# A row of attention scores by way of DRAM, and a group of transposes moved behind four additions

## The chip, the cores and the metric

The kernel runs on one core of a Trainium2 chip. The metric is the device time of one execution in microseconds; the median of three runs of the kernel before is 2945.22 us (2944.97 to 2953.04). TensorE is the matmul engine (PE in the profile), VectorE is DVE, ScalarE is ACT, GpSimd is POOL, and SyncE (SP) issues most of the transfers.

## The reference

The program is two layers over 64 graphs of 256 nodes with 256 features. Layer 0 is a graph attention network, layer 1 a relational attention with 8 heads. Everything is float32.

```python
def _gat(h, adj, W, a, F):
    Wh = h @ W
    e = leaky_relu(Wh @ a[:F] + swapaxes(Wh @ a[F:], 1, 2), 0.2)
    att = softmax(where(adj > 0, e, -9e15), axis=1)
    return att @ Wh

# layer 0
h = _gat(_gat(x, adj, W1, a1), adj, W2, a2)          # first and second attention
h = layernorm(x + h)
x = layernorm(h + relu(h @ w_ff1 + b_ff1) @ w_ff2 + b_ff2)
# layer 1
attn = softmax(q @ k.T / sqrt(32))                   # 8 heads; q, k, v projected from x
out = sum(attn * (adj == r) @ v_r for r in range(4)) @ Wo + bo
x = layernorm(x + out)
x = layernorm(x + gelu(x @ W1 + b1) @ W2 + b2)
```

The change concerns one term of the second attention: `Wh @ a[F:]` is one number for each node, and the scores need it as a row, the same in all 128 partitions, with the 512 nodes of two graphs along the free dimension.

## The kernel before

Graphs are worked on in pairs, 32 groups in all. A group's rows lie in SBUF as 128 partitions by 4 blocks of 128 nodes (two blocks for each graph). The main loop calls `turn` 32 times; a turn works on three groups at once, each at another stage: group y does its attention of layer 1 and its second feed-forward, group x its first feed-forward, and group z, two behind y, both attentions of layer 0. TensorE so always has a product of some group to do. In 30 of the 32 turns there is a group z; the first two groups go through these stages in a prologue.

The order of the instructions is written out by hand for TensorE, SP, VectorE and ScalarE inside a turn (`manual_schedule`); GpSimd's order, and the seam between two turns on VectorE, are left to the planner. Products of the feed-forwards and projections are done with seven block products in place of eight: `hidden_seven` holds the first half of a feed-forward. Its steps are named by a digit, the number of the product, and a or b, the half of the hidden blocks. A step puts a product into a PSUM bank and then takes it from there: the first product that goes to a quarter of h is copied by ScalarE (L954), the second is added by VectorE (L951). Steps c, d and s apply the Gelu to a finished quarter on ScalarE (L960); step 4 applies it straight from PSUM. `HiddenOut` holds the second half: sums of quarters on VectorE (L1020, tiles eq and eaq), then the products L1034, whose additions into y are L1042.

Around the change, the second half of a turn runs so. TensorE does the products of the second hidden layer of y. VectorE meanwhile finishes the moments of group x (L865, L866), takes the additions L951, applies a scale and a shift to y (L903, L906), and then transposes group x's normalised rows in blocks of 32 by 32 (`normed_features`, L717, four instructions). The blocks are afterwards put where they belong by twelve transfers on SP and four copies on GpSimd (L726), which gives hT, the features by nodes, of the next turn's layer 1. Only then come the last four additions of h (steps 7a, 7b, 3a, 3b).

After step 4b, `second_scores` makes the row: `score_rows` transposes a column of hp, broadcast to 128 columns, with four matmuls against the identity (L781), one for each block of nodes, into a PSUM bank. ScalarE makes the raw scores from it, one instruction for each block (L799: row plus the node's own number as the bias), VectorE the leaky step (L807), ScalarE the exponential (L810), VectorE masks and sums (L814, L818), and ScalarE scales hp (L830), which the products of the second attention (L850, ygp) use. Between these stand the output products of y: product 1, which needs a finished quarter of h, then product 5, which needs the first sum, and so on. The next turn begins with differences of hT on VectorE (L1069, tile tq) and the projections (L1102).

Pools hand out buffers: "g" has six PSUM banks, "es" two buffers in SBUF of 4 KB a partition, used by sums of exponentials (L1140) and reciprocals (L1160). `to_broadcast` reads one column many times over without copying it.

Of the kernel before, what the change touches and what calls it, by code (L numbers as in the profile page):

```python
# [9 lines left out]
F32 = mybir.dt.float32  # L10
# [6 lines left out]
P = 128  # L17
# [368 lines left out]
def narrow_path(  # L386
# [13 lines left out]
    nc = tc.nc  # L400
    B, N, F = x.shape
# [7 lines left out]
    T = G * NB  # L409
    TN = G * N  # L410
# [6 lines left out]
    const = ctx.enter_context(tc.tile_pool(name="const", bufs=1))  # L417
    io = ctx.enter_context(tc.tile_pool(name="io", bufs=2))
    work = ctx.enter_context(tc.tile_pool(name="work", bufs=2))
    psum = ctx.enter_context(tc.tile_pool(name="psum", bufs=1, space=PSUM))  # L420
    ctx.enter_context(nc.allow_non_contiguous_dma(reason="vectors, once"))

    def bank(name):
        return psum.tile([P, 512], F32, tag="g", name=name, bufs=6)


    Q = P // 32
# [255 lines left out]
    rows = work.tile([P, T, 2 * F], F32, tag="v", name="rows", bufs=1)  # L683
# [10 lines left out]
    def behind(*names):  # L694

        stack = ExitStack()
        for n in names:
            stack.enter_context(tc.issue_after(mark[n].ins))
        return stack
# [7 lines left out]
    def with_ones(hT):  # L707

        nc.gpsimd.memset(hT[KB - 1][one], 1.0)
        return hT  # L710

    def normed_features(u, l, xn, natural=False, copied=(), later=False):


        yt = work.tile([P, Q, KB, T, 32], F32, tag="yt", name=f"yt{u}_{l}", bufs=1)
        for t in range(T):
            mark["transposed"] = nc.vector.transpose(  # L717
                yt[:, :, :, t].rearrange("p q k r -> p k q r"),
                xn[:, t].rearrange("p (k q c) -> p k q c", k=KB, c=32))
        if natural:  # L720
            hT = work.tile([P, KB, TN], F32, tag="hT", name=f"hT{u}_{l}")
            to = hT.rearrange("c k (t a r) -> c (k t) a r", a=Q, r=32)
            for q in reversed(range(Q)):
                for a in range(Q):
                    move = nc.gpsimd.tensor_copy if q == a else nc.sync.dma_start
                    move(to[q * 32:(q + 1) * 32, :, a], yt[a * 32:(a + 1) * 32, q].rearrange("c k t r -> c (k t) r"))  # L726
            return with_ones([hT[:, k] for k in range(KB)])
        hT = work.tile([P, Q, KB, T, 32], F32, tag="hT", name=f"hT{u}_{l}")
        n, moves = 0, []
        for q in range(Q):  # L730
            for a in range(Q):
                to, at = hT[q * 32:(q + 1) * 32, a], yt[a * 32:(a + 1) * 32, q]
                if q == a:
                    nc.gpsimd.tensor_copy(to, at)  # L734
                else:
                    if n not in copied:
                        nc.sync.dma_start(to, at)
                    elif later:
                        moves.append((to, at))
                    else:  # L740
                        nc.scalar.copy(to, at)
                    n += 1
        hT = [hT[:, :, k].rearrange("p a t r -> p t a r") for k in range(KB)]
        return (hT, iter(moves)) if later else hT
# [32 lines left out]
    def score_rows(u, l, wh, c):  # L777

        rows = bank(f"rows{u}_{l}")
        for t in range(T):  # L780
            nc.tensor.transpose(rows[:, t * P:(t + 1) * P],  # L781
                                wh[:, t, c:c + 1].to_broadcast([P, P]), ident)
        return rows

    class Softmax:
# [83 lines left out]
    def norm(u, l, y, blocks=range(T), mv=None, rest=range(NB, T)):  # L869

        n, t0 = f"{u}_{l}_{blocks[0]}", blocks[0]
        bt = slice(t0, t0 + len(blocks))
        mv = moments(u, l, y, blocks if mv is None else rest, mv)
        rs = work.tile([P, T], F32, tag="rs", name=f"rs{n}")
        nm = work.tile([P, T], F32, tag="nm", name=f"nm{n}")
        nc.gpsimd.tensor_scalar(rs[:, bt], mv[:, bt, 1], EPS, 0.0, op0=ALU.add, op1=ALU.add)  # L876
        nc.gpsimd.tensor_tensor(rs[:, bt], rs[:, bt], mhalf[:, bt], ALU.pow)  # L877
        if l == 3:
            nc.gpsimd.tensor_add(high[:, bt], high[:, bt], mv[:, bt, 0])
        return blocks, mv, rs, nm  # L880

    def offsets(blocks, mv, rs, nm):
        bt = slice(blocks[0], blocks[0] + len(blocks))
        mark["offset"] = nc.vector.scalar_tensor_tensor(nm[:, bt], mv[:, bt, 0], -1.0, rs[:, bt], op0=ALU.mult, op1=ALU.mult)  # L884

    def applied_norm(y, blocks, mv, rs, nm, part=None, gpsimd=False):
        if part is None:
            offsets(blocks, mv, rs, nm)
        for t in part or blocks:
            if gpsimd:  # L890
                nc.gpsimd.tensor_scalar(y[:, t, :], y[:, t, :], rs[:, t:t + 1], nm[:, t:t + 1],
                                        op0=ALU.mult, op1=ALU.add)
                continue
            mark["normed"] = nc.scalar.activation(y[:, t, :], y[:, t, :], AF.Identity,  # L894
                                                  bias=nm[:, t:t + 1], scale=rs[:, t:t + 1])

    def affine(y, g_, b_):

        times(y, g_)
        plus(y, b_)  # L900

    def times(y, g_):
        nc.vector.tensor_mul(y, y, g_[:, None, :].to_broadcast(list(y.shape)))  # L903

    def plus(y, b_):
        nc.vector.tensor_add(y, y, b_[:, None, :].to_broadcast(list(y.shape)))  # L906
# [142 lines left out]
    def out_sums(u, l):  # L1049
        two = [work.tile([P, HPB, NB * N], F32, tag=t, name=f"{t}q{u}_{l}") for t in ("e", "ea")]  # L1050
        return [t[:, :, i * N:(i + 1) * N] for t in two for i in range(2)]
# [137 lines left out]
        d = g[z]  # L1189
        d["xp"] = projected(z, d["xT"], blocks, d.get("xp"))  # L1190

    def first_scores(z):
        d = g[z]
        d["m"] = Softmax(z, 0, d["xp"], score_rows(z, 0, d["xp"], F + 2), F + 3)

    def second_scores(z):
        d = g[z]
        d["m"] = Softmax(z, 1, d["hp"], score_rows(z, 1, d["hp"], F), F + 1)

    def first_softmax(z):  # L1200
        first_scores(z)
# [61 lines left out]
    def stored(u, y, bt):  # L1263
        b = slice(G * u + bt.start // NB, G * u + bt.stop // NB)
        nc.sync.dma_start(out[b].rearrange("b (c p) f -> p (b c) f", p=P), y[:, bt, :])
# [47 lines left out]
    def turn(y_, x_, z, rest=None):  # L1313
        Y, X, Z = (g.get(u) for u in (y_, x_, z))
        hT, y = Y["hT"], Y["y"]
        quads = [(b, m) for b in range(G) for m in range(KB)]
        p = Projections(y_, hT)
        q, k_, v = p.qk[:, :, 0], p.qk[:, :, 1], p.v
# [44 lines left out]
        with order:  # L1363
# [227 lines left out]
            second = hidden_seven(y_, 1, hT, w1s, b1, AF.Gelu, Y, tt.rearrange("p a n -> p (a n)"), bool(X))  # L1591
# [6 lines left out]
            if not X:  # L1598
# [2 lines left out]
                half(1)  # L1601
                second("t")
            if Z:
                second("2a 1a")
                n = norm(x_, 1, X["y"], mv=n, rest=range(NB + 1, T))
                second("2b 1b ca 6a")
                offsets(*n)
                applied_norm(X["y"], *n, [0])
                applied_norm(X["y"], *n, [2, 3], True)
                second("5a")  # L1610
                applied_norm(X["y"], *n, [1])
                affine(y, rg3, rb3)
                second("6b 5b cb")
                X["hT"] = normed_features(x_, 1, X["y"], natural=True)
                second("7a 7b sa sb 3a da 3b db 4a 4b")
            else:
                if X:
                    n = norm(x_, 1, X["y"], mv=n, rest=range(NB + 1, T))
                second("2a 1a 2b 1b" if X else "2b 1b")
                if not X:  # L1620
                    with behind("added"):
                        affine(y, rg3, rb3)
                second("5a 5b")
                if waiting:
                    times(waiting[0][1], rg4)
                second("3a 3b")
                if X:
                    offsets(*n)
                    applied_norm(X["y"], *n, [0])
                    applied_norm(X["y"], *n, [1])  # L1630
                    applied_norm(X["y"], *n, [2, 3], True)
                second("6a 6b ca cb da db 7a 7b")
                if waiting:
                    plus(waiting[0][1], rb4)
                    stored(*waiting.pop(), slice(0, T))
                if X:
                    X["hT"] = with_ones(to_features(X["y"], f"h2T{x_}", (nc.vector.tensor_copy,) * 2))
                second("sa sb 4a 4b")
            if y_ >= NG - 2:
# [5 lines left out]
                else:  # L1645
                    for _ in pieces:
                        pass
                return
            second_scores(z)
            out = HiddenOut(y_, 1, y, h1, w2s, out_sums(y_, 1))  # L1650
            out.product(1)
            out.sums(1, 2)
# [229 lines left out]
```

## Time and profile before

| What | Value |
|---|---|
| Median of three runs | 2945.22 us |
| The profiled execution's own time | 2946.93 us |
| Its span, first to last instruction | 2945.3 us |
| TensorE busy | 2921.1 us, 99% |
| VectorE busy | 2609.6 us, 89% |
| ScalarE busy | 1898.9 us, 64% |
| GpSimd busy | 624.9 us, 21% |
| Row transposes of the second attention (L781, from hp) | 128 matmuls, 19.4 us busy, all 32 groups |
| Transposes of features (L717) | 364 in all, median 402 ns |
| hT transfers behind them (L726) | 360, 609 ns of issue each |
| Granted TensorE clock | 0.998 of full speed |

A line of a group of instructions names the line of the code, the engine, the operation, the tile written and those read, the shapes and the count; after the bar come the busy time, the mean of one instruction in ns, and the idle time before them. In a timeline a line begins with the start in us from the start of the span and the time that the merged instructions cover; at its end, in brackets, stands the idle time before it and what ended it. A matmul of float32 operands is two hardware instructions, so 8 products of the code are "x16"; a transpose is one. Matmuls overlap, so a TensorE instruction's price is the distance between starts, not its duration.

### The profile page before, as it was taken

To read this page: it belongs to the slowest core of one execution; us is meant where nothing else is said; L and a number is where in the kernel's file an instruction comes from. 1 tells how busy PE (TensorE), PEld (TensorE's weight loads), DVE (VectorE), ACT (ScalarE), POOL (GpSimd) and SP (SyncE) were. 2 spreads that over 40 slices of the span, in tenths; PEclk is the share of its full clock that TensorE was granted. 3 is DMA by queue.
4 is the path that set the end of the run, shared out by engine and by line. 5 is a ranking of instruction groups with operands and counts; after the bars stand their busy time and mean duration, and the time that the engine had idled before them with its cause. 6 is when DMAs were issued, how large, how long until landed. Compare 5 with 4: busy or idle time off the path is not lost.

```text
span 2945.3 us, 58649 instructions
## 1 busy us (share of the span) xinstructions
PE 2921.1 (99%) x22206; PEld 2502.4 (85%) x22206; DVE 2609.6 (89%) x5027; ACT 1898.9 (64%) x3985; POOL 624.9 (21%) x931
## 2 busy tenths in 40 slices
PE   9999999999999999999999999999999999999998
PEld 7788888888888888888888888888888888888876
DVE  5889899988989898999889898989998898989886
ACT  5566666676666666666766766666667667666653
POOL 3312211122121122111221211221112212112210
PEclk9999999999999999999999999999999999999999
DMA  5011111111111111111111111111111111111000
GB/s 153 13 31 32 38 32 34 24 40 32 37 29 23 38 32 38 32 33 24 40 33 37 29 23 38 32 39 32 33 24 40 32 37 30 23 38 32 17 9 16
DMA packets 408020, 99.27 MB, mean 34 GB/s; under 512 B 357834, under 2 KB 407220, under 8 KB 407732
## 3 DMA queue, kind: packets, MB, share of 16 engines
q1 hardware_dynamic: 406332, 94.13, 14.8%
q8 instruction: 178, 2.92, 0.4%
q0 software_dynamic: 1056, 1.05, 0.1%
q14 instruction: 110, 0.90, 0.1%
q10 hardware_dynamic: 344, 0.28, 0.0%
HBM read 56.78 MB, written 16.78 MB: 25 GB/s over the span
## 4 chain that ended last, share of the span: by engine, by line
PE 97%; DVE 1%; ACT 1%; DMA 0%; issue 0%; POOL 0%; POOLq 0%; DVEq 0%; ACTq 0%
PE yf L1034 27%; PE h1a L942 15%; PE h1b L942 12%; PE po L1151 8%; PE v L1102 6%; PE qk L1102 6%; PE sp L1123 4%; PE hpp L839 4%; PE ygp L850 4%; PE xpp L772 4%; PE yop L850 4%; PE zo L1154 2%; PE rows L781 1%; DMA first<-in_adj_dram 0%; ACT h L960 0%
## 5 line engine op out<-in xcount | busy, mean ns | idle before, releaser
L1132 ACT ACTIVATE e<-sp 128x512 f32<-128x512 f32 x512 | 270.9, 612 | 71.2 <-issue 43.8
L1136 DVE TENSOR_TENSOR ea<-e,aT 128x1024 f32<-128x1024 f32 x256 | 310.1, 1213 | 1.6 <-ACT e L1132 1.6
L894 ACT ACTIVATE y<-y,nm,rs 128x256 f32<-128x256 f32 x442 | 235.0, 592 | 57.5 <-DVE nm L884 56.7
L951 DVE TENSOR_TENSOR h<-h1a,h 128x512 f32<-128x512 f32 x293 | 197.1, 680 | 81.4 <-PE h1a L942 81.3
L954 ACT COPY h<-h1b 128x512 f32<-128x512 f32 x293 | 175.4, 599 | 124.9 <-PE h1b L942 123.1
L960 ACT ACTIVATE h<-h,cols 128x256 f32<-128x256 f32 x512 | 222.4, 502 | 36.8 <-DVE h L951 32.5
L734 POOL COPY hT<-yt 32x256 f32<-32x256 f32 x244 | 211.3, 866 | 145.0 <-DVE yt L717 132.4
L1089 ACT COPY qk<-qk 128x512 f32<-128x512 f32 x128 | 74.3, 580 | 234.7 <-PE qk L1102 233.9
L865 DVE BATCH_NORM_STATS2 st<-y 128x6 f32<-128x256 f32 x512 | 208.6, 408 | 5.6
L876 POOL TENSOR_SCALAR rs<-mv 128x4 f32<-128x4 f32 (+1 forms) x134 | 41.5, 310 | 805.8 <-DVE mv L866 439.0
L1042 DVE TENSOR_TENSOR y<-yf,y 128x256 f32<-128x256 f32 x448 | 184.9, 413 | 29.7 <-PE yf L1034 29.7
L960 ACT ACTIVATE h<-h1a,cols 128x256 f32<-128x256 f32 x256 | 102.7, 465 | 132.4 <-PE h1a L942 132.3
L1164 POOL TENSOR_TENSOR low<-low,rq 128x16 f32<-128x16 f32 x64 | 13.9, 217 | 810.4 <-DVE rq L1163 802.6
L906 DVE TENSOR_TENSOR y<-y,rb 128x1024 f32<-128x1024 f32 x126 | 163.0, 1294 | 2.2
L1141 DVE TENSOR_TENSOR es<-e 128x1024 f32<-128x1024 f32 x128 | 155.4, 1214 | 0.0
L903 DVE TENSOR_TENSOR y<-y,rg 128x1024 f32<-128x1024 f32 x126 | 152.8, 1213 | 0.0
L877 POOL TENSOR_TENSOR rs<-rs,mhalf 128x4 f32<-128x4 f32 (+1 forms) x134 | 139.5, 1041 | 8.3
L1123 PE MATMUL sp<-qk 32*128 32x256 f32 x2048 | 138.3, 394 | 0.0
L942 PE MATMUL h1a<-tt,wf 128*128 128x256 f32 x512 | 137.6, 392 | 0.0
L1151 PE MATMUL po<-e,v 128*32 128x256 f32 x2048 | 135.5, 382 | 0.0
L1151 PE MATMUL po<-ea,v 128*32 128x256 f32 x2048 | 134.5, 379 | 0.0
L717 DVE STREAM_TRANSPOSE yt<-y 128x256 f32<-128x256 f32 x364 | 128.3, 407 | 0.9 <-ACT y L894 0.7
(288 smaller groups left out, 7728.3 us busy)
## 6 DMA issues: line engine op xcount, KB each, us to landing
hT<-yt SPq DMA_DIRECT2D x666, 32.0 KB, 1.8
y<-in_x_dram SPq DMA_DIRECT2D x32, 512.0 KB, 5.2
xq<-in_x_dram SPq DMA_DIRECT2D x240, 64.0 KB, 2.1
aq<-in_adj_dram SPq DMA_DIRECT2D x240, 64.0 KB, 2.2
out_dram<-y SPq DMA_DIRECT2D x30, 512.0 KB
wf<-in_L_gnn_w_ff_dram SPq DMA_DIRECT2D x2, 1024.0 KB, 8.5
w<-in_L_gnn_W_dram SPq DMA_DIRECT2D x2, 1024.0 KB
first<-in_adj_dram POOLq DMA_DIRECT2D x2, 512.0 KB, 9.7
```

The costliest lines, as they stand in the source:

```text
L734: nc.gpsimd.tensor_copy(to, at)
L850: nc.tensor.matmul(ps[:, i * F:(i + 1) * F], lhs(t, k), rhs(b, k), start=(k == 0), stop=(k == n - 1))
L865: nc.vector.bn_stats(st[:, t, :], y[:, t, :])
L894: mark["normed"] = nc.scalar.activation(y[:, t, :], y[:, t, :], AF.Identity, bias=nm[:, t:t + 1], scale=rs[:, t:t + 1])
L942: nc.tensor.matmul(ps[:, i * N:(i + 1) * N], w_[:, f * P:(f + 1) * P], m, start=first and i == 0, stop=True, skip_group_check=True)
L960: nc.scalar.activation(y, y if ps is None else ps[:, i * N:(i + 1) * N], func, bias=bi[:, f:f + 1])
L1034: nc.tensor.matmul(s.ps[n][:, i * F2:(i + 1) * F2], a[:, k, i * P:(i + 1) * P], w_[:, k, :], start=n in (1, 2, 5) and i == 0 and k == 0, s ...
L1102: nc.tensor.matmul(ps[:, i * N:(i + 1) * N], l, r, start=n in (1, 2, 5) and i == 0, stop=True, skip_group_check=True)
L1123: nc.tensor.matmul(ps[a][:, j * N:(j + 1) * N], k_[hp, m, j0:j0 + P], q[hp, m, b * N:(b + 1) * N], start=True, stop=True)
L1132: nc.scalar.activation(e[:, a, :], ps[a], AF.Exp, scale=isd)
L1136: nc.vector.tensor_tensor(ea[:, a:a + 2, :], e[:, a:a + 2, :], ab[:, None, :].to_broadcast([P, 2, NB * N]), ALU.mult)
L1151: nc.tensor.matmul(po[hp, m * N:(m + 1) * N], vs[:, hp], w[:, a, j * N:(j + 1) * N], start=(n == 0), stop=(n == len(terms) - 1))
```

## The change

The second attention's row no longer comes from TensorE. A new helper, `line_rows`, is called at the beginning of the second hidden layer of y, one hidden layer earlier than the row is used. One VectorE transpose turns the column of hp, broadcast to 32, in blocks of 32 by 32, so that partitions 0, 32, 64 and 96 each hold 32 nodes of every block. A transfer writes these to a line in DRAM in 16 pieces of 128 bytes, in the order of the nodes; a second reads the line back into all 128 partitions. The row is then a tile in SBUF from the pool's "es" buffers, and `second_scores` takes it in place of making its own. The prologue's two groups, and the first attention of all groups, still use `score_rows`.

The second part moves `normed_features` of group x, its four transposes with their twelve transfers and four copies, from before step 7a to after step 3b, behind the last addition of h.

```diff
+    dram = ctx.enter_context(tc.tile_pool(name="dram", bufs=2, space=bass.MemoryType.DRAM))
...
+    def line_rows(u, l, wh, c):
+        line = dram.tile([T, Q, 32], F32, tag="line", name=f"line{u}_{l}")
+        rows = work.tile([P, TN], F32, tag="es", name=f"rows{u}_{l}")
+        turned_ = rows[:, :T * 32].rearrange("p (t r) -> p t r", r=32)
+        nc.vector.transpose(turned_, wh[:, :, c:c + 1].to_broadcast([P, T, 32]))
+        nc.sync.dma_start(line.rearrange("t q r -> q t r"), turned_[::32])
+        nc.sync.dma_start(rows, bass.AP(tensor=line.tensor, offset=line.offset, ap=[[0, P], [1, TN]]))
+        return rows
...
-    def second_scores(z):
+    def second_scores(z, rows=None):
         d = g[z]
-        d["m"] = Softmax(z, 1, d["hp"], score_rows(z, 1, d["hp"], F), F + 1)
+        d["m"] = Softmax(z, 1, d["hp"], score_rows(z, 1, d["hp"], F) if rows is None else rows, F + 1)
...
             if Z:
+                rows1 = line_rows(z, 1, Z["hp"], F)
                 second("2a 1a")
...
                 second("6b 5b cb")
+                second("7a 7b sa sb 3a da 3b db")
                 X["hT"] = normed_features(x_, 1, X["y"], natural=True)
-                second("7a 7b sa sb 3a da 3b db 4a 4b")
+                second("4a 4b")
...
-            second_scores(z)
+            second_scores(z, rows1)
```

More of the change, by code (lines that the diff above doesn't have):

```diff
@@ L1190, in project, with first_scores @@
         d["xp"] = projected(z, d["xT"], blocks, d.get("xp"))
-    def first_scores(z):
+    def first_scores(z, rows=None):
         d = g[z]
-        d["m"] = Softmax(z, 0, d["xp"], score_rows(z, 0, d["xp"], F + 2), F + 3)
-    def second_scores(z):
+        d["m"] = Softmax(z, 0, d["xp"], score_rows(z, 0, d["xp"], F + 2) if rows is None else rows, F + 3)
+    def second_scores(z, rows=None):
         d = g[z]
-        d["m"] = Softmax(z, 1, d["hp"], score_rows(z, 1, d["hp"], F), F + 1)
+        d["m"] = Softmax(z, 1, d["hp"], score_rows(z, 1, d["hp"], F) if rows is None else rows, F + 1)
     def first_softmax(z):
```

## The prediction

> **What bounds the kernel now.** I read the page first: busy shares, then the chain that ended last, then the row transposes' own group.
>
> ```profile
> PE 2921.1 (99%) x22206; PEld 2502.4 (85%) x22206; DVE 2609.6 (89%) x5027; ACT 1898.9 (64%) x3985; POOL 624.9 (21%) x931
> ...
> PE 97%; DVE 1%; ACT 1%; DMA 0%; issue 0%; POOL 0%; POOLq 0%; DVEq 0%; ACTq 0%
> ```
>
> ```profile
> L781 PE MATMUL rows<-ident,hp 128*128 128x128 f32 x128 | 19.4, 273 | 0.1
> ```
>
> TensorE is the chain. Whatever leaves its queue is gained unless it then waits. The 273 ns of a row transpose is its latency; they overlap, so the price must be read from distances. For that I took the timeline of one turn in the middle, engine by engine. TensorE, around the four row transposes:
>
> ```profile
> 1417.31 1.89 PE L942 MATMUL h1a<-tt,w 128*128 128x256 f32 x8
> 1419.04 1.89 PE L942 MATMUL h1b<-hT,w1s 128*128 128x256 f32 x8
> 1420.77 1.89 PE L942 MATMUL h1a<-tt,w 128*128 128x256 f32 x8
> 1422.49 0.60 PE L781 MATMUL rows<-ident,hp 128*128 128x128 f32 x4
> 1422.93 1.95 PE L1034 MATMUL yf<-w,h 128*128 128x128 f32 x16
> 1424.72 1.95 PE L1034 MATMUL yf<-w2t,eq 128*128 128x128 f32 x16
> ```
>
> The first three lines are steps 7, 3 and 4 of the second hidden layer (a and b each); then the row; then output products 1 and 5. There is no gap. VectorE, ScalarE and the transfer queue in the same stretch:
>
> ```profile
> 1411.53 0.18 DVE L866 BATCH_NORM_AGGREGATE mv<-st 128x2 f32<-128x6 f32 x1
> 1412.40 0.69 DVE L951 TENSOR_TENSOR h<-h1a,h 128x512 f32<-128x512 f32 x1 [0.70 <-PE h1a L942]
> ...
> 1416.53 1.47 DVE L906 TENSOR_TENSOR y<-y,rb 128x1024 f32<-128x1024 f32 x1
> 1417.92 1.41 DVE L717 STREAM_TRANSPOSE yt<-y 128x256 f32<-128x256 f32 x4
> 1419.26 1.24 DVE L951 TENSOR_TENSOR h<-h1a,h 128x512 f32<-128x512 f32 x2
> 1420.43 1.26 DVE L951 TENSOR_TENSOR h<-h1b,h 128x512 f32<-128x512 f32 x2
> 1423.27 1.23 DVE L1020 TENSOR_TENSOR eq<-h 128x1024 f32<-128x1024 f32 x1 [1.57 <-ACT h L960]
> ```
>
> ```profile
> 1419.94 3.30 ACT L960 ACTIVATE h<-h,cols 128x256 f32<-128x256 f32 x8 [1.04 <-DVE h L951]
> 1423.14 1.53 ACT L960 ACTIVATE h<-h1a,cols 128x256 f32<-128x256 f32 x4
> 1424.57 1.56 ACT L799 ACTIVATE s<-rows,hp 128x256 f32<-128x256 f32 x4
> ```
>
> ```profile
> 1409.92 0.39 SPq L441 DMA_DIRECT2D y<-in_x_dram  x1
> 1419.39 8.35 SPq L726 DMA_DIRECT2D hT<-yt  x12
> 1429.75 5.32 SPq L449 DMA_DIRECT2D aq<-in_adj_dram  x8
> ```
>
> The reader should see a chain that almost touches TensorE: the transposes (L717) hold back the four additions of h, these hold back the eight Gelus, and these the first sum (L1020, eq), which ends at 1424.50. Product 5 takes that sum as its stationary operand: its weight load starts at 1424.61, its matmul at 1424.72. The shortest distance in this trace from a VectorE end to a weight load that waited for it is 0.055 us, so only about 0.06 us are spare.
>
> **What the skill says.** TensorE: Matmul & The Clock Gate, LDWEIGHTS, prices a load by its columns over 1.2, so 107 ns for 128. The trace agrees: four rows take 0.44 us from first start to the next product's start, 109 ns each. SBUF — State Buffer, Who interferes with whom: a VectorE instruction with two SBUF inputs and a GpSimd one that reads SBUF exclude each other, and the first to issue keeps the port. The trace agrees: L906 takes 1.47 us where it starts while a GpSimd normalisation runs, and 1.22 us alone; a GpSimd copy of hT takes 0.39 us alone and 1.27 us under a VectorE product. DMA: Bandwidth & Descriptors, Anatomy of one DMA, gives about 2.0 us fixed for a transfer (its fit is for another issuing engine); here 32 KB lands 1.8 us after issue.
>
> **Removed.** 30 turns times four row transposes (first attention keeps its own, as do the two groups of the prologue): 30 x 0.44 = 13.1 us of TensorE. The row's PSUM bank is no longer taken; the built order shows no later tile waiting on a worse bank.
>
> **Added.** (a) One VectorE transpose of 128x128, the first thing behind the moments at 1411.7. Not in the trace: half of a 128x256 one gives 0.17 (1.34 us for four, start to next start), all of it 0.40; I take 0.25. It falls into the 0.70 us in which VectorE waits for TensorE; at 0.40 it still fits. Without that cover it would delay the additions by its length. hp is complete by 1409.2 (the copies L841), so it waits for nothing, and queued behind it is only an addition that TensorE releases at 1412.40. (b) Two transfers on SP, the second waiting on the queue for the first to land. Behind them stand only the features' twelve, far later. Write: from 1412.1, 2 to 3 us (3 if behind the 512 KB of y, which lands at about 1415.1). Read: 256 KB, between 1.8 (32 KB) and 5.2 us (512 KB), by interpolation 3.4, plus 0.6 of issue. Landing between 1417 and 1420. (c) The four raw scores read SBUF in place of PSUM: Gelus take 502 ns from SBUF (L960 h<-h) and 465 from PSUM, so 4 x 0.04 = 0.15 us of ScalarE.
>
> **Moved.** The four transposes stand behind the last addition. Absolute times, with all before 1417 unchanged: additions follow the ends of their products by 0.10: 1418.44, 1419.30, 1420.17, 1421.03 (the last three-b product ends at 1420.93). The first three come up to 0.8 us earlier, the last one not at all. Gelus: the last pair starts 0.04 behind the last addition, at 1421.73, and ends at 1422.6, so 0.6 earlier. VectorE: addition 1421.03 + 0.60 + transposes 1.34 = 1422.97, when the first sum starts (in place of 1423.27; ScalarE no longer decides). It ends 1.22 later, at 1424.19; weight load 1424.25, matmul 0.10 behind it, 1424.35. TensorE, 0.44 us earlier, would want it at 1424.28. So a wait of 0.07 us appears; with 0.05 us for a start that is not quite tight, 0.13. I take 0.10.
>
> Behind it: GpSimd's four copies of hT now meet the sums. The first sum has issued first; the second sum and the leaky step may lose 0.1 to 0.25 each. What stands behind has room: product 3's sum ends at 1428.75 for a load at 1430.0, s3 at 1429.9 for 1431.7, and the scaled hp of the second attention come earlier, since the built order puts the four sums of the next turn (L1069) behind product 7's addition and no longer ahead of the reciprocal. ScalarE begins the raw scores at 1423.96, behind the last Gelus. The twelve hT transfers issue from 1423.0 to 1431.4 and land by 1432.7; L1069 comes at about 1434.7, TensorE's first use at 1438.5. Adjacency then loads until about 1437; its user is early in the next turn's second half.
>
> **Sum.** Per turn 0.44 - 0.10 = 0.34; 30 turns: 10.2 us (their row transposes start 89.96 us apart, once 90.18). Against the profiled execution: span 2945.3 to 2935.1, with 1.6 us around it (its own time 2946.93). The median of the runs, 2945.22, is 1.7 below that time; the same step from it gives 2935.0.
>
> **Rivals.**
> No wait at product 5: if the sum starts 0.1 us sooner, all 13.1 us are kept: 2932.1. For it: all terms are within hundredths. Against: the last addition is fixed by TensorE and the transposes must fit.
> A larger wait: the first sum starts 0.1 to 0.2 us later than worked out, by slower transposes or by a GpSimd copy that gets the port first; then 0.2 to 0.33 us of 0.44 go back, leaving 3.3 to 7.2 us: 2938 to 2942. For it: a transpose beside GpSimd took 0.43 in place of 0.40. Against: the copies need the last transpose, and the sum is already at the head of VectorE's queue.
> The row arrives late: slower. Place: ScalarE's first raw score at 1423.96. From there the masks and the scaled hp lead to the second attention's matmul (1433.65 now) with about 0.5 us to spare. A landing after about 1424.8 eats the gain, one after 1425.1 makes it slower by 0.3%, and each us more costs 30: landing at 1426 gives about 2980. That needs a round trip of 13 to 14 us against 5 to 8 worked out; nothing else is on the queue then.
> That the row's matmuls stay in place is excluded by the built program.
>
> **How the numbers follow.** Forecast 0.50 (2933.9 to 2936), no wait 0.17, larger wait 0.27, late row 0.06. A change under 0.3%, 8.8 us, is about what a measurement here can't tell from none. Forecast and no wait lie beyond it: faster 0.67; larger wait: same 0.27; late row: slower 0.06. Range 2931.5 to 2940.5: it holds the forecast, the full gain and most of the larger wait.
>
> **What would show it.** Row matmuls of hp on TensorE only for the first two groups; product 1 following step 4b directly; eq starting some 1.9 us after the last h1b addition, with the L717 group between; a wait for eq ahead of product 5 of about 0.1 us; the turn at 89.62; hT's issues ending some 4 us later with nobody waiting. Wrong if raw scores wait for a transfer, if L1069 does, or if the turn shortens by under 0.29 us.

## The result, and the profile after

The changed kernel takes 2934.64 us, the median of six runs (2932.34 to 2936.58). The kernel before took 2945.95 us in the same comparison. The ratio is 0.9959, with a 95% interval of 0.9949 to 0.9969. The interval lies below 1, so the changed kernel is faster, by 0.4%; the forecast was 2935.0.

Line numbers move with the change: L781 is now L782, L717 is L718, L726 is L727, L799 is L811, L807 is L819, L906 is L918, L942 is L954, L951 is L963, L960 is L972, L1020 is L1032, L1034 is L1046 and L1042 is L1054. The new helper's transpose is L792, its write L793, its read L794.

The page of the changed kernel: busy shares, the chain that ended last, and one group of GpSimd (busy us, mean ns of one, then the idle time before it).

```profile
PE 2906.7 (99%) x22086; PEld 2490.4 (85%) x22086; DVE 2625.7 (90%) x5057; ACT 1908.1 (65%) x3985; POOL 699.7 (24%) x931
...
PE 97%; DVE 1%; ACT 1%; DMA 0%; issue 0%; POOL 0%; POOLq 0%; DVEq 0%; ACTq 0%
...
L727 POOL COPY hT<-yt 32x256 f32<-32x256 f32 x120 | 124.9, 1041 | 145.0 <-PE h1a L954 136.0
```

TensorE has 120 matmuls fewer, 30 turns by four, and is still the chain. VectorE and ScalarE work 16 and 9 us more, GpSimd 75 us more, and none of that shows in the time.

The instructions that write or read the row, by tile (count, then shortest, median and longest ns, first and last start):

```profile
L782 PE MATMUL rows<-ident,hp x8: 272/273/322, 30.4 to 60.8; 128*128 128x128 f32 x8
...
L811 ACT ACTIVATE s<-rows,hp x128: 465/512/518, 31.4 to 2760.5; 128x256 f32<-128x256 f32 x128
L792 DVE STREAM_TRANSPOSE rows<-hp x30: 277/278/279, 149.7 to 2747.0; 128x128 f32<-128x128 f32 x30
```

The eight remaining row matmuls from hp are those of the prologue's two groups. VectorE's transpose, which the trace before did not have, takes 0.278 us.

Now the same stretch of a turn as before the change. TensorE's timeline:

```profile
1410.99 1.89 PE L954 MATMUL h1b<-hT,w1s 128*128 128x256 f32 x8
1412.72 1.89 PE L954 MATMUL h1a<-tt,w 128*128 128x256 f32 x8
1414.44 1.95 PE L1046 MATMUL yf<-w,h 128*128 128x128 f32 x16
1416.23 1.99 PE L1046 MATMUL yf<-w2t,eq 128*128 128x128 f32 x16
1418.06 1.95 PE L1046 MATMUL yf<-w,h 128*128 128x128 f32 x16
```

From the start of step 4 to the start of product 1 it is now 1.72 us, where it was 2.16 us (1420.77 to 1422.93): the 0.44 us of the row are gone. From product 5 (w2t,eq) to the product behind it the distance is 1.83 us in place of the undisturbed 1.79: a wait of about 0.04 us has come, too short for the view to name.

VectorE, ScalarE, GpSimd and the transfer queue:

```profile
1403.58 0.28 DVE L792 STREAM_TRANSPOSE rows<-hp 128x128 f32<-128x128 f32 x1
1404.36 0.69 DVE L963 TENSOR_TENSOR h<-h1a,h 128x512 f32<-128x512 f32 x1 [0.50 <-PE h1a L954]
...
1412.92 0.69 DVE L963 TENSOR_TENSOR h<-h1b,h 128x512 f32<-128x512 f32 x1 [0.17 <-PE h1b L954]
1413.53 1.41 DVE L718 STREAM_TRANSPOSE yt<-y 128x256 f32<-128x256 f32 x4
1414.86 1.18 DVE L1032 TENSOR_TENSOR eq<-h 128x1024 f32<-128x1024 f32 x1
1416.08 1.31 DVE L1032 TENSOR_TENSOR eq<-eq,h 128x1024 f32<-128x1024 f32 x1
1417.31 0.88 DVE L819 SCALAR_TENSOR_TENSOR s<-s 128x512 f32<-128x512 f32 x1
```

```profile
1414.46 1.55 ACT L972 ACTIVATE h<-h1a,cols 128x256 f32<-128x256 f32 x4
1415.89 1.70 ACT L811 ACTIVATE s<-rows,hp 128x256 f32<-128x256 f32 x4
```

```profile
1415.06 4.32 POOL L727 COPY hT<-yt 32x256 f32<-32x256 f32 x4 [4.68 <-PE h1a L954]
```

```profile
1403.88 0.58 SPq L793 DMA_DIRECT2D line<-rows  x1
1406.00 0.34 SPq L794 DMA_DIRECT2D rows<-line  x1
1415.00 7.85 SPq L727 DMA_DIRECT2D hT<-yt  x12
```

The row's transpose lies in VectorE's gap, which shrank from 0.70 to 0.50 us. The read of the row is issued 2.1 us behind the write. The raw scores (L811) begin at 1415.89, right behind the last Gelus, and wait for no transfer. The features' transposes (L718) now follow the last addition of h at once, and the first sum (eq<-h) follows the transposes.

**Where the time went.** A turn, measured between the starts of product 1, lasted 89.96 us (one of 29 distances 90.18) and now lasts 89.56, in 29 of 29 distances. That is 0.40 us, 0.44 less 0.04, and 30 turns make 12.0 us. The two profiled executions' own times, 2946.93 and 2932.34 us, lie 14.6 apart, but 2.6 of that come before the first of these marks (at 163.2 and 160.6 us). The time up to this mark ran from 160.6 to 172.5 us over the twelve profiled executions of this study, so the turns are the cleaner measure, and the experiments are judged by them. The medians lie 11.3 us apart.

### The profile page after: what moved, and what is told of

It reads as the page before. It is cut to its first block, busy times and chain, and to the rows that moved or that the text cites. A ratio compares the mean times of both kernels' runs of the same rounds, so it can differ in the third digit from the quotient of the medians.

```text
span 2930.7 us, 58588 instructions
## 1 busy us (share of the span) xinstructions
PE 2906.7 (99%) x22086; PEld 2490.4 (85%) x22086; DVE 2625.7 (90%) x5057; ACT 1908.1 (65%) x3985; POOL 699.7 (24%) x931
## 4 chain that ended last, share of the span: by engine, by line
PE 97%; DVE 1%; ACT 1%; DMA 0%; issue 0%; POOL 0%; POOLq 0%; DVEq 0%; ACTq 0%
PE yf L1046 27%; PE h1a L954 15%; PE h1b L954 12%; PE po L1163 8%; PE v L1114 6%; PE qk L1114 6%; PE sp L1135 4%; PE hpp L851 4%; PE ygp L862 4%; PE xpp L773 4%; PE yop L862 4%; PE zo L1166 2%; PE rows L782 0%; DMA first<-in_adj_dram 0%; ACT h L972 0%
## 5 line engine op out<-in xcount | busy, mean ns | idle before, releaser
L963 DVE TENSOR_TENSOR h<-h1a,h 128x512 f32<-128x512 f32 x293 | 201.5, 688 | 94.4 <-PE h1a L954 94.4
L906 ACT ACTIVATE y<-y,nm,rs 128x256 f32<-128x256 f32 x442 | 235.0, 591 | 57.2 <-DVE nm L896 56.4
L735 POOL COPY hT<-yt 32x256 f32<-32x256 f32 x244 | 211.3, 866 | 144.6 <-PE v L1114 90.9
L972 ACT ACTIVATE h<-h,cols 128x256 f32<-128x256 f32 x512 | 226.2, 503 | 13.9 <-DVE h L963 9.6
L1054 DVE TENSOR_TENSOR y<-yf,y 128x256 f32<-128x256 f32 x448 | 183.6, 410 | 29.2 <-PE yf L1046 29.2
L972 ACT ACTIVATE h<-h1a,cols 128x256 f32<-128x256 f32 x256 | 103.2, 468 | 132.3 <-PE h1a L954 132.2
L918 DVE TENSOR_TENSOR y<-y,rb 128x1024 f32<-128x1024 f32 x126 | 163.4, 1297 | 3.2
L727 POOL COPY hT<-yt 32x256 f32<-32x256 f32 x120 | 124.9, 1041 | 145.0 <-PE h1a L954 136.0
L889 POOL TENSOR_TENSOR rs<-rs,mhalf 128x4 f32<-128x4 f32 (+1 forms) x134 | 139.8, 1043 | 8.3
L954 PE MATMUL h1a<-tt,wf 128*128 128x256 f32 x512 | 137.6, 392 | 0.0
```

The source lines that it names most:

```text
L954: nc.tensor.matmul(ps[:, i * N:(i + 1) * N], w_[:, f * P:(f + 1) * P], m, start=first and i == 0, stop=True, skip_group_check=True)
L972: nc.scalar.activation(y, y if ps is None else ps[:, i * N:(i + 1) * N], func, bias=bi[:, f:f + 1])
```

## The experiments

The theory: per turn the row's 0.44 us are won, less the wait that the moved transposes bring at product 5. The rivals: the kernel would have gained as much or more by one part alone; or the other effects of the change (transfers, GpSimd's longer copies, later features) cost something too. The table is a summary. The turn is the median of the 29 distances, for the late row their range (in some of the runs one to three single turns are 0.1 to 0.5 us longer); the other times in us are relative to the start of output product 1 of the second layer.

| Kernel | Turn | First sum, start to end | Product 5, weight load |
|---|---|---|---|
| before | 89.96 | 0.34 to 1.57 | 1.68 |
| after | 89.56 | 0.42 to 1.60 | 1.72 |
| row alone | 89.96 | 0.78 to 2.00 | 2.12 |
| move alone | 89.96 | -0.02 to 1.16 | 1.68 |
| both, row matmuls kept | 89.96 | -0.02 to 1.16 | 1.68 |
| transposes behind the first sum | 90.45 | 0.14 to 1.36 | 1.67 |
| late row | 91.58 to 92.23 | 0.61 to 1.80 | 1.91 |

### The row alone

The features' transposes stay where they were in the kernel before. Against the changed kernel:

```diff
-                second("7a 7b sa sb 3a da 3b db")
                 X["hT"] = normed_features(x_, 1, X["y"], natural=True)
-                second("4a 4b")
+                second("7a 7b sa sb 3a da 3b db 4a 4b")
```

> The row by way of DRAM, the features' transposes left where they were. Theory (TensorE's 0.44 us a turn are gained only as far as the first sum is ready): VectorE's first sum still ends 2.00 us behind step 4b, TensorE now wants it 0.44 us earlier and waits 0.37 us for it, so 0.06 us a turn are left: turn 89.90, about 2 us in all, ratio 0.999. Rival (the row alone brings the gain, the move is an accessory): turn 89.56, ratio 0.996, as with both parts.

Measured: 2948.04 us against 2948.58, ratio 0.9992 (0.9981 to 1.0002); the turn is 89.96, as before. TensorE, its weight loads, and VectorE in the timeline:

```profile
1420.36 1.89 PE L954 MATMUL h1a<-tt,w 128*128 128x256 f32 x8
1422.09 1.95 PE L1046 MATMUL yf<-w,h 128*128 128x128 f32 x16
1424.24 2.02 PE L1046 MATMUL yf<-w2t,eq 128*128 128x128 f32 x16 [0.20 <-DVE eq L1032]
```

```profile
1424.21 1.86 PEld L1046 LDWEIGHTS yf<-w2t,eq 128*128 128x128 f32 x16 [0.36 <-PE yf L1046]
```

```profile
1422.87 1.23 DVE L1032 TENSOR_TENSOR eq<-h 128x1024 f32<-128x1024 f32 x1 [1.57 <-ACT h L972]
```

The row's 0.44 us leave between step 4 and product 1 (1.73 us), and come back whole at product 5, whose weight load starts 2.12 us behind product 1 in place of 1.68. The first sum is held by the Gelus (L972), which are held by the additions, and these by the features' transposes. It ends at 1424.10, and the weight load follows 0.11 us later. So the change's second part is needed. The expectation left 0.06 us a turn; nothing was left, so the kernel before had no time to spare at product 5 at all.

### The move alone

The kernel before, with only the features' transposes moved; its row comes from TensorE.

```diff
                 second("6b 5b cb")
+                second("7a 7b sa sb 3a da 3b db")
                 X["hT"] = normed_features(x_, 1, X["y"], natural=True)
-                second("7a 7b sa sb 3a da 3b db 4a 4b")
+                second("4a 4b")
```

> The features' transposes behind the additions, the row left to TensorE's four transposes. Theory: the sum comes earlier, but TensorE did not wait for it: turn 89.96, ratio 1.000. Rival (the move is what brings the gain, by earlier additions and Gelus): turn about 89.6, ratio 0.996.

Measured: 2947.29 against 2948.58 us, ratio 0.9999 (0.9989 to 1.0009); turn 89.96. The first sum ends 0.41 us earlier than before and nobody gains by it, since TensorE had no wait there to lose. The move costs nothing by itself either: GpSimd's slower copies and the later transfers delay no one.

### Both parts, with the row's matmuls kept

The changed kernel, with the four row transposes of TensorE put back as work that nobody uses.

```diff
+            score_rows(z, 1, Z["hp"], F)
             second_scores(z, rows1)
```

> Both parts, and beside them the four row transposes left on TensorE with their result unused. Theory (the gain is TensorE's time in the queue): all of it is given back, turn 89.96, ratio 1.000. Rival (the gain comes from the row lying in SBUF, from ScalarE's earlier raw scores or from the PSUM bank that is freed): turn about 89.6.

Measured: 2950.68 against 2948.58 us, ratio 1.0005 (0.9995 to 1.0016); turn 89.96. The turn loses 0.40 us again, and the first sum stands at the same place as in the move alone. The DRAM line, its 30 reads of 256 KB and the later features thus neither cost nor save time; all of the gain is the four matmuls' place on TensorE. In the changed kernel itself 0.44 less 0.04 is the whole 0.40 us of the turn, which leaves nothing for them there either.

### The features' transposes between the two sums

Would the last 0.04 us be won by putting the transposes behind the first sum?

```diff
-                second("7a 7b sa sb 3a da 3b db")
-                X["hT"] = normed_features(x_, 1, X["y"], natural=True)
-                second("4a 4b")
+                second("7a 7b sa sb 3a da 3b db 4a 4b")
...
-            out.sums(1, 2)
+            out.sums(1)
+            X["hT"] = normed_features(x_, 1, X["y"], natural=True)
+            out.sums(2)
```

> As the changed kernel, but the features' transposes behind the first of the two sums. Theory: the last wait, about 0.03 us ahead of product 5, is gone: turn 89.52 to 89.53, 1 us less than the changed kernel, not to be told apart by times but by the turn in the trace. Rival (something behind it becomes late: the second sum or the addition ahead of product 6, or hT): turn longer than 89.56.

The theory of this expectation was missed, and its rival came: 2960.05 us, ratio 1.0040 (1.0027 to 1.0053), turn 90.45. Product 5 waits no more (load at 1.67), but the second sum comes 0.98 us later on VectorE, and the additions behind it 0.9 to 1.1 us later. TensorE and VectorE in the timeline:

```profile
1435.05 1.98 PE L1046 MATMUL yf<-w,eaq 128*128 128x128 f32 x16
1437.67 2.05 PE L1046 MATMUL yf<-w,eaq 128*128 128x128 f32 x16 [0.64 <-DVE y L1054]
```

```profile
1437.20 0.41 DVE L1054 TENSOR_TENSOR y<-yf,y 128x256 f32<-128x256 f32 x1
```

The second of these products is product 7, which writes into the PSUM bank of product 6 and so waits until VectorE has added that one into y. The addition ends at 1437.61 and the product starts 0.06 us later, 2.62 us behind its predecessor in place of 1.79: 0.83 us lost. In the changed kernel the same addition ends at 8.64 on the relative scale, and product 7 starts at 8.97. There were thus some 0.3 us of room between the two, and the addition's 1.06 us of delay (it ends at 9.70) overran them.

### The row late

The row's transpose and transfers behind the last addition of h in place of ahead of the hidden layer.

```diff
             if Z:
-                rows1 = line_rows(z, 1, Z["hp"], F)
                 second("2a 1a")
...
                 second("7a 7b sa sb 3a da 3b db")
+                rows1 = line_rows(z, 1, Z["hp"], F)
                 X["hT"] = normed_features(x_, 1, X["y"], natural=True)
```

> As the changed kernel, but the row's transpose and its two transfers only behind the last addition of h, ahead of the features' transposes, so 10 us later. Theory: the row has more than 6 us to spare in the changed kernel and costs nothing there; here it lands 4 to 5 us behind step 4b in place of 4 us ahead of it, the raw scores wait about 3 us for it, and with 0.5 us to spare at the second attention's products TensorE loses 2 to 3 us a turn: turn 91.6 to 92.6, 3000 to 3025 us. Rival (the row's arrival stands nowhere near the path, the second attention has room for it): turn under 90.

A single execution: 3008.55 us beside 2945.68; turns of 91.58 to 92.23. In the list of waits (us in total, times, longest):

```profile
ACT s L811 <- DMA rows<-line: 87.6, 30, 3.4
```

ScalarE waits 2.9 us in each turn; the raw scores start 2.9 to 3.5 us later than in the changed kernel (4.31 to 4.95 against 1.44), and the turn grows by 2.0 to 2.7 us. The sizes are those expected, but the place is not. One turn, TensorE and VectorE:

```profile
1460.95 1.95 PE L1046 MATMUL yf<-w,h 128*128 128x128 f32 x16
1463.53 2.05 PE L1046 MATMUL yf<-w2t,eq 128*128 128x128 f32 x16 [0.64 <-DVE y L1054]
1465.60 2.05 PE L1046 MATMUL yf<-w,eaq 128*128 128x128 f32 x16
1468.09 2.05 PE L1046 MATMUL yf<-w,eaq 128*128 128x128 f32 x16 [0.44 <-DVE y L1054]
1469.98 2.32 PE L862 MATMUL ygp<-hp,s 128*128 128x256 f32 x10
```

```profile
1462.45 0.69 DVE L819 SCALAR_TENSOR_TENSOR s<-s 128x512 f32<-128x512 f32 x1 [2.17 <-ACT s L811]
1463.06 0.42 DVE L1054 TENSOR_TENSOR y<-yf,y 128x256 f32<-128x256 f32 x1
```

The leaky step (L819) waits for the raw scores at the head of VectorE's queue, and the addition of product 1 (1463.06) stands behind it. Product 6 (1463.53) writes into the bank that this addition frees, and starts 2.58 us behind its predecessor in place of 1.79. Products 3 and 7 (the two w,eaq lines) lose 0.28 and 0.70 us more, because the sum and the addition that they need stand in the same queue. The second attention's product (ygp), where the expectation put the loss, follows product 7 by 1.89 us, the distance behind every product here that had waited for its bank; it adds no wait of its own. And 0.19 us of the growth arise ahead of all this: the row's transpose now stands before the features' transposes, so product 5's load starts at 1.91 in place of 1.72. So the row's landing does decide once it is late, by way of VectorE's queue; that the turn came out as expected, by another path, is luck. This is the rival of the prediction that ends on the slower side, and the early place of `line_rows` is what keeps it away: there, the row is in SBUF more than 6 us before it is used, if the read takes the 3.1 us that the page of a later run gives for it.

### Both rows from VectorE

If the trick pays 0.40 us for the second attention, does it pay for the first one's row too (`score_rows` from xp, the other 128 matmuls)? Its row is wanted earlier, so product 1 of the first layer's output was put between the two products of the attention's output (L862, the expectation's L850), to win time.

```diff
-                    project(z, range(1, 2))
+                    project(z, range(1, T))
...
-                    out.sums(1, 2)
+                    out.sums(1)
+                    rows0 = line_rows(z, 0, Z["xp"], F + 2)
+                    out.sums(2)
...
-                project(z, range(T // 2, T))
+                out.product(1)
...
-                first_scores(z)
+                first_scores(z, rows0)
...
-                out(1)
+                out.add(1)
```

> As the changed kernel, and the first attention's row by way of DRAM too: projections of blocks 2 and 3 moved up behind block 1, output product 1 of the first feed-forward between the two products L850 in their place, the row's VectorE transpose behind the first sum (L1032). Theory (row matmuls are worth their 0.44 us a turn as far as nothing else becomes late): turn 89.12 if the scaled xp still arrive ahead of the first attention's product (hpp), which has about 0.5 us to spare and a VectorE chain ahead of it that the move makes up to 0.7 us later; so 89.1 to 89.4, ratio to the kernel before 0.991 to 0.994. Rival (the wait moves to hpp and eats all): 89.56 or more.

And the same order with the first row still on TensorE, to part the order from the row (the diff is the one above without the lines of rows0):

> The reordering of the run with both rows, with the first attention's row left to TensorE. Theory: the reordering by itself is neutral, turn 89.5 to 89.7. Rival: it delays hpp or the second product L850, turn over 89.8.

Both expectations were missed: 2957.85 us (ratio 1.0042, 1.0026 to 1.0059) and 2958.63 us (1.0043, 1.0029 to 1.0058), and the turn is 90.37 us in both. With both rows, TensorE and VectorE in the first layer's output:

```profile
1493.43 3.74 PE L1046 MATMUL yf<-wf2t,eq 128*128 128x128 f32 x32
1497.88 2.05 PE L1046 MATMUL yf<-wf,eaq 128*128 128x128 f32 x16 [0.71 <-DVE y L1054]
```

```profile
1497.41 0.42 DVE L1054 TENSOR_TENSOR y<-yf,y 128x256 f32<-128x256 f32 x1
```

With the order alone, TensorE:

```profile
1493.67 3.74 PE L1046 MATMUL yf<-wf2t,eq 128*128 128x128 f32 x32
1497.67 2.05 PE L1046 MATMUL yf<-wf,eaq 128*128 128x128 f32 x16 [0.27 <-DVE y L1054]
```

The first wf,eaq product is product 3, which takes product 5's bank. Products 5 and 6 (x32) need 3.57 us undisturbed; product 3 starts 4.45 us behind them with both rows and 4.00 with the order alone. The waits are 0.88 and 0.43 us: the 0.44 us of the row went into this one wait, to within 0.01. The addition of product 5 is late in both. Both runs lose a further 0.37 us between the starts of product 3 and product 4 (7.43 us in place of 7.06): product 3 reaches its successor 0.10 us late, and product 7 waits 0.17 us for the third sum and does the same. The rival of the first expectation named a loss of this size at another place, the first attention's product (hpp). Why VectorE comes late to the addition is tested next.

### The rows early, and the addition of product 5 first

In the run with both rows VectorE had idle times of 0.72, 0.28 and 0.47 us around the products of the attention's output. The next kernel fills these: adjacency, raw scores and the addition of product 1 stand earlier.

```diff
                     out.sums(2)
             if Z:
+                early_adjacency(z)
                 shares(1)
...
             if Z:
-                early_adjacency(z)
+                first_scores(z, rows0)
+                Z["m"].scores(0)
+                Z["m"].scores(1)
+                out.add(1)
             elif X:
...
-                first_scores(z, rows0)
...
-                out.add(1)
-                Z["m"].scores(0)
-                Z["m"].scores(1)
                 Z["m"].exp(0)
```

> Both rows come from VectorE and a DRAM line, and output product 1 of the first layer stands between the two projection products, as in the run with both rows; in addition the early adjacency products stand directly behind the second pair of output sums, and the first attention's raw scores and the addition of product 1 stand ahead of the second part of the attention's output, so that they fall into the 1.6 us in which VectorE had been idle there. If that idle time was what made VectorE's chain late in the run with both rows, the third sums come some 1.5 us sooner, products 6 and 7 no longer wait, and the turn is between 89.1 (the full second 0.44 us) and 89.3 us: 2920 to 2927 us. If VectorE has no room there at all (90% busy), the work put earlier only delays the sums behind it, products 5 or 6 wait as before, and the turn is 89.6 us or more, up to 90.4: 2936 to 2960 us.

Measured: 2955.34 against 2946.70 us, ratio 1.0029 (1.0020 to 1.0039), turn 90.16. Better than both rows by 0.21 us a turn, but still slower than the kernel before, so the better of the two expectations was missed. VectorE and TensorE:

```profile
1491.88 1.19 DVE L1032 TENSOR_TENSOR eaq<-h,eq 128x1024 f32<-128x1024 f32 x1
1494.31 0.16 DVE L896 SCALAR_TENSOR_TENSOR nm<-mv,rs 128x4 f32<-128x4 f32 x1 [1.24 <-POOL rs L889]
...
1495.41 0.42 DVE L1054 TENSOR_TENSOR y<-yf,y 128x256 f32<-128x256 f32 x1
```

```profile
1491.65 3.74 PE L1046 MATMUL yf<-wf2t,eq 128*128 128x128 f32 x32
1495.89 2.05 PE L1046 MATMUL yf<-wf,eaq 128*128 128x128 f32 x16 [0.50 <-DVE y L1054]
```

Now VectorE is on time until 1493.07, and then stands 1.24 us for GpSimd's reciprocal root (L889) with the small step of a normalisation (L896). The addition of product 5 is queued behind it. By this reading VectorE was not too full; one early wait stood ahead of a release, that is, of an instruction that another engine waits for. Two kernels test it by putting the addition first:

```diff
                 out.sums(4)
-                offsets(*n)
                 out(2)
-                applied_norm(y, *n, range(T))
                 Z["m"].masks(0)
                 out(5)
+                offsets(*n)
+                applied_norm(y, *n, range(T))
                 Z["m"].masks(1)
```

One of the two also puts the third sum ahead of the features' transposes:

```diff
                 out.product(6)
+                out.sums(3)
                 hT = normed_features(y_, 2, y, copied=(1, 2, 4, 5, 7, 8, 10, 11))
...
                 out.add(6)
-                out.sums(3)
                 out(3)
```

> As the run with the rows early, with two more moves on VectorE in the first layer's output: the addition of product 5 and the second pair of masks' first half stand ahead of the normalisation's small step (which waits 1.24 us for GpSimd), and the third sum stands ahead of the features' transposes. Theory: what held TensorE in the run with the rows early was the order on VectorE, first the addition of product 5 (it ended 1495.83 there; product 3 takes its bank and would have wanted it by about 1495.1), then the third sum (ended 1499.62; product 7 would have wanted it by 1498.8). With both moved, the addition ends at about 1494.5 and the sum at about 1496.7 on that scale, neither waits any more, and the turn is between 89.1 and 89.3 us: 2920 to 2927 us. Rival: VectorE is simply too full with both rows (its busy share there over 95%), what is put ahead of one wait makes the next one late, and the turn stays at 89.6 us or more: 2936 us or more.

> The same without the third sum's move: only the addition of product 5 stands ahead of the normalisation's small step. Theory: product 3 no longer waits (0.67 us won), but the third sum still stands behind the features' transposes and ends at about 1499.6 on the scale of the run with the rows early, some 0.8 us behind product 7's wish, so product 7 waits for what product 3 no longer does: turn 89.9 to 90.2 us. Rival (VectorE too full anyhow): about the same turn as with the third sum moved.

Measured, with the sum moved too: 2928.19 against 2945.28 us, ratio 0.9931 (0.9917 to 0.9946), turn 89.28. Without: a single execution, 2928.65 us, turn 89.27 to 89.28. Busy shares and the read of the row (count, KB each, us from issue to landing) on the page of the first, then its timeline:

```profile
PE 2901.5 (99%) x21966; PEld 2481.6 (85%) x21966; DVE 2629.5 (90%) x5087; ACT 1904.0 (65%) x3985; POOL 719.1 (25%) x931
...
rows<-line SPq DMA_DIRECT2D x60, 256.0 KB, 3.1
```

```profile
1479.82 3.62 PE L1046 MATMUL yf<-wf2t,eq 128*128 128x128 f32 x31
1483.28 1.95 PE L1046 MATMUL yf<-wf,eaq 128*128 128x128 f32 x16
```

```profile
1481.05 0.42 DVE L1054 TENSOR_TENSOR y<-yf,y 128x256 f32<-128x256 f32 x1
...
1482.07 0.42 DVE L1054 TENSOR_TENSOR y<-yf,y 128x256 f32<-128x256 f32 x1
1482.41 0.15 DVE L896 SCALAR_TENSOR_TENSOR nm<-mv,rs 128x4 f32<-128x4 f32 x1
```

The addition of product 5 ends at 1482.49, product 3 follows its predecessors with no wait named, and by 1482.41 GpSimd's root is there, so VectorE no longer stands for it. The turn is 0.28 us shorter than that of the changed kernel and in the range expected; the time lies a little above its 2920 to 2927 us. It is the fastest kernel of the study. Of the second row's 0.44 us 0.16 is still lost, between the starts of products 3 and 7 (1483.28 to 1486.97, 3.69 us in place of 3.53): the first attention's product, which lies between them, now waits for ScalarE's scaled xp (L842). No run has this order with the first row left on TensorE, so what the order alone would give is not shown. On the third sum the expectation was missed: without its move the turn was to be 89.9 to 90.2, and it was the same 89.28. VectorE, which no longer stands 1.24 us, comes to that sum in time anyhow: it ends 0.23 us ahead of the start of product 7. The theory held for the addition, and the rival, a VectorE too full, fell: its share is 89% in the kernel that loses and 90% in the one that wins.

## Why the prediction was right

The forecast, 0.34 us a turn and 2935.0, met 0.40 us a turn and 2934.64. That the times agree to 0.4 us is in part luck: the turns gave 1.8 us more than forecast, and the kernel before had a median of 2945.95 us in this comparison in place of 2945.22, with the rest within the runs' spread. By the prediction's steps:

**The row removed**: 0.44 us per turn by the distance of starts, not the 273 ns of one matmul. Shown, by 2.16 to 1.72 us on TensorE here, and by the run with the matmuls kept.

**The wait at product 5**: the mechanism was right, place and order of events too, and the size was off: 0.04 us came in place of 0.10. Two terms were mis-sized, in opposite senses. The sum came too late in the prediction: it started 0.42 us behind product 1, not 0.48, since the last addition of h came 0.07 us earlier than worked out, and took 1.18, not 1.22. And the load of product 5 came too early in it: it follows the sum's end not after 0.055 us, read as the shortest distance in the trace (which is in fact 0.044; most are 0.053), but after 0.11 to 0.12 (1424.10 to 1424.21 in the row alone; 1.60 to 1.72 here). With the measured terms the sum of the prediction is 0.42 + 1.18 + 0.12 = 1.72, against 1.68 that TensorE would like. The 0.05 us added "for a start that is not quite tight" had no cause, and 0.07 and 0.05 make 0.12, not 0.13; the 0.10 taken stands between.

**"Only about 0.06 us are spare"**: none were. The load in the kernel before, then in the changed one:

```profile
1424.61 1.86 PEld L1034 LDWEIGHTS yf<-w2t,eq 128*128 128x128 f32 x16
```

```profile
1416.16 1.86 PEld L1046 LDWEIGHTS yf<-w2t,eq 128*128 128x128 f32 x16
```

Before, it starts 1.68 us behind product 1, which is the sum's end, 1.57, and 0.11. The move alone, with the sum 0.41 us earlier, starts it at 1.68 too, so this is TensorE's own pace. The row alone shows it again, since 0.44 us came back whole.

**The moved transposes**: the additions were predicted at -4.05, -3.19, -2.32 and -1.46 us on this scale and came at -4.05, -3.18, -2.39 and -1.53. So they hang on TensorE alone now, as worked out: VectorE's waits for TensorE at the additions of h, over both layers, are 99.6 us in all (94.4 for h1a and 5.2 for h1b) in place of 81.3.

**The row's new way**: the transpose took 0.278 us, for 0.25 taken between bounds of 0.17 and 0.40, and is hidden. Write and read take 2.1 + 3.1 us from the write's issue to the landing where the page names a landing (the kernel with both rows and the addition first), within the 5 to 8 us given; some 12 us were there. The Trainium skill (DMA: Bandwidth & Descriptors, Anatomy of one DMA) gives about 2.0 us fixed for a transfer on another path, most of it until the write is known to have landed; the 2.1 us from the issue of the write to that of the read that waits for it agree. The raw scores cost 1.70 us in place of 1.56, 0.14 for a predicted 0.15.

**What stands behind "has room"**: true at the changed kernel's delays, and too broad as it was told. Product 3's sum, s3 and hp were named; the tightest release, the addition of product 6 ahead of product 7, was not. Delayed by 1.06 us, it was the first to fall, in the run with the transposes between the sums.

**GpSimd**: the four copies of hT met the sums as foreseen. They take 4.32 us in place of 1.71, the second sum 1.31 for 1.23 and the leaky step 0.88 for 0.69. That agrees with the Trainium skill (SBUF — State Buffer, Who interferes with whom): a VectorE instruction with two SBUF inputs and a GpSimd one that reads SBUF exclude each other, and who issues first keeps the port. TensorE waits for neither: behind product 5 its output products follow each other at 1.79 us, as before.

**The rivals**: no wait at all (2932.1) and a larger one (2938 to 2942) stand on either side of what came, and the late row was shown to be real by making it late. Its size fits: with the 0.5 us to spare that the prediction named, 2.9 us of delay give 2.4 a turn, and 2.0 to 2.7 were measured. Its path does not: the prediction led it through the masks and the scaled hp to the second attention's product, and the loss stood before that, at products 6, 3 and 7, by way of the additions that queue on VectorE behind the leaky step. That the size agrees all the same is luck.

## What to carry to other kernels

When TensorE is the chain, taking work out of its queue pays only as far as the next release keeps pace: work out for each product behind it which instruction of another engine it needs, and when that one ends, down to a tenth of a us. Look not at how full the other engine is but at what stands ahead of the release in its queue; here one small step that waited for GpSimd cost 0.9 us a turn by its place (90.16 to 89.28), and moving it turned a loss into the best kernel. Ask the same of a transfer that comes late: the late row held TensorE not where its scores are used last, but through an addition queued behind the first of them. The row's way over DRAM cost nothing where its 5.2 us were started 12 us before the use.

## What the runs showed of the hardware that was not expected

- The weight load of product 5 started 0.11 to 0.12 us behind the end of VectorE's sum, where most weight loads that the profile puts down to VectorE start 0.053 us behind it. The reason stays open: the row alone's view names TensorE as the last to be waited for, but its product 1 ends at 1424.04, before the sum does at 1424.10. A product that waited for its PSUM bank only started 0.05 to 0.06 us behind the addition that freed it (1437.61 to 1437.67; 1497.83 to 1497.88; 1495.83 to 1495.89). Its successor then started 1.89 us behind it in place of 1.79 (1468.09 to 1469.98 with the late row), so such a wait cost 0.10 us more than the distance ahead of the product shows.
- GpSimd's four copies of hT (32x256) took 393 ns each in the kernel before and 1041 ns in the mean under VectorE's sums.
- One of ScalarE's raw scores took 512 ns from SBUF where it took 477 from PSUM.
